# Layer 0's attention: one norm a slot earlier, two keys' products in slot 0, and the last mask turned inside the last projection

## The chip, the cores and the metric

The kernel runs on one core of a Trainium2 chip. A core has five engines that run side by side, each working through its own instructions in order: TensorE (PE in the profile; PEld are its weight loads), VectorE (DVE), ScalarE (ACT), GpSimd (POOL), and SyncE (SP), which here only issues DMA transfers. Engines wait for each other through semaphores. [...]

The metric is the device time of one execution in microseconds. For the kernel before, three runs were timed: 1245.64, 1251.21 and 1258.18 us, the median 1251.21.

## The reference, cut to what matters

A two-layer perceiver on 64 batches of 32 latent rows of 256 numbers. Each layer is a cross attention, an attention and a feed-forward part, each added to x. The change touches layer 0's attention and the work that is laid beside it: the choice of blocks for layer 0's feed-forward part, and that part's first group.

```python
def _L0_attn_ref(x, g_norm, Wq, Wkv, Wout, g_out):
    ...
    xn = _layernorm(x, g_norm)
    q = xn @ Wq
    kv = xn @ Wkv
    k, v = (kv[..., :DIM_HEAD], kv[..., DIM_HEAD:])
    q = q.reshape(B, N, HEADS, DIM_HEAD).transpose(0, 2, 1, 3)
    q = _l2norm(q * SCALE)
    k = _l2norm(k)
    ...
    sim = jnp.einsum('bhid,bjd->bhij', q, k)
    attn = jax.nn.softmax(sim.astype(jnp.float32), axis=-1).astype(sim.dtype)
    out = jnp.einsum('bhij,bjd->bhid', attn, v)
    out = out.transpose(0, 2, 1, 3).reshape(B, N, HEADS * DIM_HEAD)
    out = out @ Wout
    return _layernorm(out, g_out)

def _L0_ffn_ref(x, Wr, br, W1, W2):
    ...
    prob = jax.nn.softmax(xf @ Wr.T + br, axis=-1)
    _, idx = jax.lax.top_k(prob, TOP_K)
    mask = mask.at[jnp.arange(n)[:, None], idx].set(1.0)
    h = jnp.einsum('nf,ibf->nib', xf, W1b)
    h = jax.nn.gelu(h, approximate=False) * mask[:, :, None]
    y = jnp.einsum('nib,fib->nf', h, W2b)
    ...

x = x + _L0_xattn_ref(_layernorm(x, axis=-1), ctx_512, ...)
x = x + _L0_attn_ref(_layernorm(x, axis=-1), ...)
x = x + _L0_ffn_ref(_layernorm(x, axis=-1), ...)
```

There are 16 heads of 128; the mask keeps 4 of 16 blocks of 64 hidden units for each row.

## The kernel before

The 2048 rows of x lie in SBUF as 16 tiles `xs[0]` to `xs[15]` of 128 rows, in four groups of four (g = 0 to 3). Everything is float32. The program runs in stages, and each stage opens its own pools of SBUF and PSUM and closes them at its end: stage A (layer 0's cross attention), stage B (layer 0's attention, pools wB, psB and psB2), stage C (the rest of layer 0's feed-forward part and the weights of layer 1's cross attention, pools wC and psC), and the later ones. Pools that outlive a stage are const, xnp (four buffers of one normed tile, tag "xn"), xtp, small and mbp (the masks as they are multiplied).

In stage B the order on TensorE, VectorE, ScalarE and GpSimd is the order of the code; in stage C this holds for TensorE and ScalarE only, and the compile step orders the rest, as it orders SP's transfers everywhere here.

Stage B is a loop over slots t = 0 to 16. Slot t does, for tile t: `similar` (scores `Sb` and squared lengths `ssb`, L806 and L814, then a square root), `scale` (a reciprocal on VectorE, L828, and a product), `power` (exp on ScalarE, L834), `share` (the sum over the keys `denb` on TensorE, L840, then the reciprocal L842 and the product that makes `pTb`), and for tile t - 1: `gather` (`avb`, L853, needs pTb), `project` (16 heads, each one product of the output weights, `yb`, L866), `norm_stats` and `norm_out` (L884 to L886: VectorE reads yb in PSUM and writes `yn`, GpSimd multiplies by the gain and adds to x). Between them stand numbered places 0, 1, 2, 5, 3, 4 in this order; `at(slot, place, fn)` hangs further work there:

- `query_part` (places 0 to 3): the queries of later tiles, `qb`, L775, copied out by ScalarE.
- `keys_norm`, `keys_turn`, `keys_of`, `turn_keys` for group g: the normed latents, turned (`tp_b` into `xT_b`), multiplied by the key and value weights in two halves of two tiles (`kvp`, L340, copied and squared by ScalarE), and the keys turned (`kTp`).
- `choose_norm`, `choose_turn`, `choose_blocks`, `choose_best`, `choose_store` for groups 0 to 2: the choice of blocks. `choose_best` makes the mask on VectorE in four rounds of small operations; `choose_store` turns it with four transposes (`mTp`, L627), copies it to SBUF (`mTc`, L629) and stores it to DRAM (`maskd`, L630), from where `spread` reads it broadcast.
- `ln_group(0, "c")`, `ff_begin`, `ff_hidden`, `ff_output`: the first group of the feed-forward part. `ln_group` takes the statistics of four tiles on VectorE (two instructions a tile), a square root on ScalarE, and with act=True scales the tiles on ScalarE (L190).

Places 2 and 5 stand ahead of `project`; place 5 is behind `power`, and `share` is behind `project`. In slot 16 there is no new tile: it projects and norms tile 15 among the last feed-forward outputs of group 0. Last, `write_pad(t)` in every slot fills a part of a DRAM buffer with 1040 KB from the tile `pad`. After the loop `choose_store(2)` runs as step (17, 2).

Stage C begins with `hidden(1, 0)`: products `hp` (L644) into PSUM, gelu on ScalarE (L651) into `hc`, multiplied by the mask on VectorE (L652). The weights of layer 1's cross attention (`d_q` first, L1028) are loaded at its start.

Of the kernel before, what the change touches and what calls it, by code (L numbers as in the profile page):

```python
# [7 lines left out]
F32 = mybir.dt.float32  # L8
# [5 lines left out]
P = 128  # L14
B, S, D = 64, 32, 256
NT = B * S // P
NG = NT // 4
# [28 lines left out]
def perceiver_kernel(ctx: ExitStack, tc: tile.TileContext, a: dict, out: bass.AP):  # L46
# [3 lines left out]
    const = ctx.enter_context(tc.tile_pool(name="const", bufs=1))  # L50
    xtp = ctx.enter_context(tc.tile_pool(name="xtp", bufs=2))
    xnp = ctx.enter_context(tc.tile_pool(name="xnp", bufs=4))
# [14 lines left out]
    def sm(name, shape):  # L67
        return small.tile(shape, F32, tag=name.split("_")[0], name=name)
# [97 lines left out]
    def stats(mv_slot, src, name):  # L166
        st = sm(f"lnb_{name}", [P, 6])
        nc.vector.bn_stats(st, src)
        nc.vector.bn_aggr(mv_slot, st)

    def ln_scale(mv, name, twice=False, power=False):

        rs = rstd_of(mv, 4, name, power)
        if twice:

            v2 = sm(f"lnw_{name}", [P, 4, 2])
            nc.vector.tensor_tensor(v2[:, :, 1], mv[:, :, 1], rs, ALU.mult)
            nc.vector.tensor_tensor(v2[:, :, 1], v2[:, :, 1], rs, ALU.mult)
            rs2 = rstd_of(v2, 4, f"{name}b", power)
            nc.vector.tensor_tensor(rs2, rs2, rs, ALU.mult)  # L180
            rs = rs2
        sh = sm(f"lnh_{name}", [P, 4])
        nc.vector.scalar_tensor_tensor(sh, mv[:, :, 0], -1.0, rs, ALU.mult, ALU.mult)
        return rs, sh

    def ln_out(x_, rs, sh, i, name, act=False):

        y = xnp.tile([P, D], F32, tag="xn", name=f"xn_{name}_{i}")
        if act:
            nc.scalar.activation(  # L190
                y, x_, AF.Identity, scale=rs[:, i : i + 1], bias=sh[:, i : i + 1]
            )
        else:
            nc.vector.scalar_tensor_tensor(
                y,
                x_,
                rs[:, i : i + 1],
                sh[:, i : i + 1].to_broadcast([P, D]),
                ALU.mult,
                ALU.add,  # L200
            )
        return y

    def ln_group(g, name, twice=False, act=False, power=False):

        mv = sm(f"lnm_{name}{g}", [P, 4, 2])
        for i in range(4):
            stats(mv[:, i, :], xs[4 * g + i], f"{name}{g}_{i}")
        rs, sh = ln_scale(mv, f"{name}{g}", twice, power)
        return [ln_out(xs[4 * g + i], rs, sh, i, f"{name}{g}", act) for i in range(4)]  # L210
# [114 lines left out]
    def keys_norm(g):  # L325
        latT[g] = ln_group(g, "b", twice=True, act=True, power=g == 0)

    def keys_turn(g, ps):
        latT[g] = transposed(latT[g], ps, g, "b", gain=gn)

    def keys_of(g, ps, part):

        xT = latT[g]
        if part == 0:
            keys[g] = kvp.tile([P, 4, D], F32, tag="kv", name=f"kvb{g}"), sm(f"ssk_b{g}", [P, 4])
        kv, ssk = keys[g]
        for i in range(2 * part, 2 * part + 2):
            kv_ps = ps.tile([P, D], F32, tag="mm", name=f"kvp{g}_{i}")
            for k in range(KC):
                nc.tensor.matmul(  # L340
                    kv_ps,
                    xT[:, k, i * P : (i + 1) * P],
                    b_kv[:, k, :],
                    start=(k == 0),
                    stop=(k == KC - 1),
                )
            nc.scalar.copy(kv[:, i, :], kv_ps)
            junk = kvp.tile([P, P], F32, tag="junk", name=f"junkb{g}_{i}")
            nc.scalar.activation(junk, kv[:, i, :P], AF.Square, accum_out=ssk[:, i : i + 1])
        if part == 1:  # L350
            sk = sm(f"sk_b{g}", [P, 4])
            nc.scalar.activation(sk, ssk, AF.Sqrt, bias=keps, scale=1.0 / 16.0)
            rk = sm(f"rk_b{g}", [P, 4])
            nc.vector.reciprocal(rk, sk)
            for i in range(4):
                nc.vector.tensor_scalar_mul(kv[:, i, :P], kv[:, i, :P], rk[:, i : i + 1])
            keys[g] = kv
# [13 lines left out]
    with tc.tile_pool(name="wA", bufs=2) as work, tc.tile_pool(  # L371
        name="psA", bufs=1, space=PSUM
    ) as ps1, tc.tile_pool(
        name="psA2", bufs=2, space=PSUM
# [128 lines left out]
        def project(t):  # L503
            oT = ctxo.pop(t)
            y_ps = ps1.tile([P, D], F32, tag="o", name=f"ya{t}")
            for k in range(KC):
                nc.tensor.matmul(
                    y_ps, oT[:, k, :], a_o[:, k, :], start=(k == 0), stop=(k == KC - 1)
                )
            nc.vector.tensor_add(xs[t], xs[t], y_ps)  # L510
# [50 lines left out]
    def choose_norm(g, act=True):  # L561
        choice[g] = ln_group(g, "r", act=act)
# [59 lines left out]
    def choose_store(g, ps, work):  # L622

        mask = choice.pop(g)[2]
        mT_ps = ps.tile([16, 512], F32, tag="mm", name=f"mTp{g}")
        for i in range(4):
            nc.tensor.transpose(mT_ps[:, i * P : (i + 1) * P], mask[:, i, :], ident)  # L627
        mT = work.tile([16, 512], F32, tag="mT", name=f"mTc{g}", bufs=1)
        nc.vector.tensor_copy(mT, mT_ps)  # L629
        nc.sync.dma_start(maskd[g], mT)  # L630

# [94 lines left out]
    with tc.tile_pool(name="wB", bufs=2) as work, tc.tile_pool(  # L726
        name="psB", bufs=1, space=PSUM
# [134 lines left out]
        def project(t):  # L862
            oT = ctxo.pop(t)
            y_ps = outs[t] = ps1.tile([P, D], F32, tag="y", name=f"yb{t}")
            for h in range(NH):
                nc.tensor.matmul(  # L866
                    y_ps, oT[:, h, :], b_o[:, h, :], start=(h == 0), stop=(h == NH - 1)
                )

        def norm_stats(t):  # L870
            mv = sm(f"lnm_bo{t}", [P, 1, 2])
            stats(mv[:, 0, :], outs[t], f"bo{t}")
            ve = sm(f"lnv_bo{t}", [P, 1])
            nc.vector.tensor_scalar_add(ve, mv[:, :, 1], EPS)
            sd = sm(f"lns_bo{t}", [P, 1])
            nc.scalar.activation(sd, ve, AF.Sqrt)
            outs[t] = outs[t], mv, sd

        def norm_out(t):
            y_ps, mv, sd = outs.pop(t)  # L880
            rs = sm(f"lnr_bo{t}", [P, 1])
            nc.vector.reciprocal(rs, sd)
            yn = work.tile([P, D], F32, tag="yn", name=f"ynb{t}")
            nc.vector.tensor_scalar(yn, y_ps, mv[:, 0, 0:1], rs, ALU.subtract, ALU.mult)  # L884
            nc.gpsimd.tensor_tensor(yn, yn, vec[:, V_GOUT : V_GOUT + D], ALU.mult)
            nc.gpsimd.tensor_tensor(xs[t], xs[t], yn, ALU.add)  # L886
# [20 lines left out]
        steps = {}  # L907

        def at(slot, place, fn):
            steps.setdefault((slot, place), []).append(fn)  # L910

        for g in range(1, NG):
            at(4 * g - 4, 2, lambda g=g: keys_turn(g, ps2))
            at(4 * g - 3, 1, lambda g=g: keys_of(g, ps2, 0))
            at(4 * g - 3, 3, lambda g=g: keys_of(g, ps2, 1))
            at(4 * g - 2, 2, lambda g=g: turn_keys(g, ps2))
            if g > 1:
                at((3, 6)[g - 2], 5, lambda g=g: keys_norm(g))
        for g in range(NG - 1):
            at(4 * g + 5, 5, lambda g=g: choose_norm(g))  # L920
            at(4 * g + 6, 1, lambda g=g: choose_turn(g, ps2, work))
            at(4 * g + 7, 5, lambda g=g: choose_blocks(g, ps2, work))
            at(4 * g + 7, 5, lambda g=g: choose_best(g, work, (0, 1)))
            at(4 * g + 8, 5, lambda g=g: choose_best(g, work, (2, 3)))
            at(4 * g + 9, 2, lambda g=g: choose_store(g, ps2, work))
        ff, late = {}, []

        def ff_late():
# [21 lines left out]

        at(10, 4, lambda: ff.update(mb=spread(0)))
        at(16, 2, lambda: ff.update(mb1=spread(1)))
        at(11, 5, lambda: ff.update(xn=ln_group(0, "c", act=True)))
        at(12, 2, ff_begin)
        for f, (slot, place) in enumerate(
            ((13, 2), (13, 3), (14, 0), (14, 1), (14, 2), (14, 3), (15, 0), (15, 1))
# [7 lines left out]
        for t in range(NT + 1):  # L964
# [25 lines left out]
            if t > 0:  # L990
                project(t - 1)
                norm_stats(t - 1)
# [4 lines left out]
            if t > 0:  # L997
                norm_out(t - 1)
# [7 lines left out]
            write_pad(t)  # L1006
            if t in (2, 4):
                load_c(t // 4)
        for step in steps.get((NT + 1, 2), ()):
            step()  # L1010
        xT_c1 = ff["xT1"]


# [7 lines left out]
    with tc.tile_pool(name="wC", bufs=2) as work, tc.tile_pool(  # L1021
        name="psC", bufs=2, space=PSUM
# [150 lines left out]
        for g in range(1, NG):  # L1173
# [4 lines left out]
            if g == 1:  # L1178
                mb = spread(2)
                xn = ln_group(2, "c", power=True)  # L1180
# [3 lines left out]
            if g == 3:  # L1184
                xn = ln_group(0, "d", power=True)
# [31 lines left out]
    with mbw, wd1:  # L1217
# [3 lines left out]
        with tc.tile_pool(name="wD", bufs=2) as work, tc.tile_pool(  # L1221
            name="psD", bufs=1, space=PSUM
        ) as ps1, tc.tile_pool(
            name="psD2", bufs=2, space=PSUM
# [217 lines left out]
            steps, lat = {}, {}  # L1442
# [299 lines left out]
    with tc.tile_pool(name="wE", bufs=2) as work, tc.tile_pool(  # L1742
        name="psE", bufs=1, space=PSUM
# [7 lines left out]
        ps2 = ps1  # L1751
# [439 lines left out]
```

## Time and profile before

| What | us |
|---|---|
| median of three runs | 1251.21 |
| lowest, highest | 1245.64, 1258.18 |
| the profiled execution | 1262.62 |
| its span (first to last instruction) | 1260.7 |

| Stretch of the span (us) | what runs | TensorE busy (us) | granted clock |
|---|---|---|---|
| 0 to 139 | loads, stage A | 126.75 | 0.94 |
| 139 to 505 | stage B | 352.05 | 0.97 |
| 505 to 644 | stage C | 133.34 | 0.93 |
| 644 to 981 | layer 1's cross attention | 328.86 | 0.99 |
| 981 to 1122 | layer 1's attention and routing | 114.55 | 0.77 |
| 1122 to 1260.7 | layer 1's feed-forward part | 131.06 | 0.99 |

The slots of stage B begin where TensorE starts `Sb` for a tile: 151.99 (slot 0), 168.76, 190.52, 208.95, 226.94, 246.27, 267.87 (slot 6), 287.74, 307.51, 326.84, 348.88 (slot 10), 368.74, 388.52 (slot 12), 413.49, 432.41 and 453.25 (slot 15).

In the profile a line of a timeline gives start, duration, engine, code line, operation, what it writes and reads, the shape, and in brackets how long the engine had been idle before and what ended that. "Granted clock" is the share of TensorE's full clock that was let through, averaged over the stretch. A line of waits gives who waited for whom, the total, the number of times and the longest.

### The profile page before, as it was taken

What the parts mean: (1) busy time and instruction counts of PE and PEld (TensorE: products, weight loads), DVE (VectorE), ACT (ScalarE), POOL (GpSimd) and SP (SyncE); (2) the same over time, 40 slices, a digit from 0 to 9 for tenths busy, and PEclk for the clock granted to TensorE, in tenths of its full rate; (3) what the DMA queues carried; (4) which work ended last, traced back from release to release, by engine and by line L of the source; (5) the groups of instructions that cost most, each with busy time, mean ns of one, the idle gap of its engine ahead of it and who ended that gap; (6) DMA issues with size and microseconds to landing.
All of it is one profiled execution on the core that took longest, in us unless ns stands there. A gap on an engine that the chain in (4) does not pass through costs nothing. (4 is left out here: it accounts for less than half of the span.)

```text
span 1260.7 us, 26257 instructions
## 1 busy us (share of the span) xinstructions
PE 1186.6 (94%) x10187; PEld 832.7 (66%) x10187; DVE 775.8 (62%) x1885; ACT 557.9 (44%) x1305; POOL 368.6 (29%) x472
## 2 busy tenths in 40 slices
PE   8999999999999999999989999999999788789997
PEld 5656767677776557578667777776766466655664
DVE  5766247678869866443257777677775455665333
ACT  2437344464544541221346656565655355331111
POOL 2333326675766563100010000000010356332111
PEclk9989989999998989998989999999999888689999
DMA  5121124554463452832051111121200244211110
GB/s 148 42 70 36 28 76 118 157 155 119 119 185 108 116 165 76 257 104 63 25 116 31 47 37 47 39 53 30 53 1 1 94 145 162 66 39 56 43 33 10
DMA packets 94973, 103.11 MB, mean 82 GB/s; under 512 B 37792, under 2 KB 71329, under 8 KB 94626
## 3 DMA queue, kind: packets, MB, share of 16 engines
q1 hardware_dynamic: 92978, 97.19, 27.0%
q0 software_dynamic: 1872, 4.23, 1.0%
q8 instruction: 82, 1.34, 0.4%
q14 instruction: 41, 0.34, 0.1%
HBM read 69.45 MB, written 32.85 MB: 81 GB/s over the span
## 5 line engine op out<-in xcount | busy, mean ns | idle before, releaser
L1362 ACT ACTIVATE pp<-Sd,nm 128x257 f32<-128x257 f32 x256 | 118.0, 474 | 66.7 <-DVE nm L1358 61.4
L775 PE MATMUL qb<-xT_b,b_q 128*128 128x256 f32 x512 | 125.4, 394 | 0.0
L775 PEld LDWEIGHTS qb<-xT_b,b_q 128*128 128x128 f32 x512 | 97.4, 195 | 41.4 <-issue 20.9
L866 PE MATMUL yb<-b_o,oTb 128*128 128x256 f32 x512 | 116.4, 386 | 0.0
L866 PEld LDWEIGHTS yb<-b_o,oTb 128*128 128x128 f32 x512 | 98.6, 194 | 14.4 <-issue 0.7
L1358 DVE TENSOR_REDUCE nm<-Sd 128x2 f32<-128x514 f32 x128 | 83.1, 686 | 23.1 <-PE Sd L1350 23.1
L1371 DVE TENSOR_TENSOR pp<-pp,rd 128x514 f32<-128x514 f32 x128 | 89.0, 695 | 2.1
L1393 ACT COPY pTd<-pt 128x512 f32<-128x512 f32 x112 | 61.4, 598 | 49.6 <-PE pt L1387 49.6
L794 POOL TENSOR_TENSOR q2b<-qTb 128x512 f32<-128x512 f32 x64 | 65.2, 1046 | 28.2 <-ACT qTb L783 18.5
L1410 PE MATMUL od<-pTd,na 128*64 128x256 f32 x480 | 65.3, 392 | 5.6 <-issue 4.3
L783 ACT COPY qTb<-qb 128x512 f32<-128x512 f32 x64 | 37.4, 584 | 73.1 <-PE qb L775 71.5
L1350 PE MATMUL Sd<-ct,qTd 64*128 64x257 f32 x480 | 68.3, 403 | 0.0
L1387 PE MATMUL pt<-cst,pp 128*128 128x128 f32 x512 | 67.4, 275 | 0.0
L1387 PEld LDWEIGHTS pt<-cst,pp 128*128 128x128 f32 x512 | 59.4, 142 | 9.9 <-issue 5.6
L1148 PE MATMUL qd<-xT_d,d_m 128*128 128x256 f32 x256 | 65.3, 399 | 0.2 <-ACT xT_d L242 0.2
L828 DVE RECIPROCAL rqb<-rqb 128x512 f32<-128x512 f32 x16 | 53.5, 3343 | 17.8 <-ACT rqb L823 17.8
L657 PE MATMUL yc<-c,hc 128*128 128x256 f32 x256 | 59.7, 389 | 2.7 <-DVE hc L652 2.7
L1426 PE MATMUL yd<-d_n,co 128*128 128x256 f32 x256 | 59.5, 386 | 0.0
L1148 PEld LDWEIGHTS qd<-xT_d,d_m 128*128 128x128 f32 x256 | 47.2, 194 | 17.2 <-issue 6.0
L842 DVE RECIPROCAL rdb<-denb 128x512 f32<-128x512 f32 x16 | 53.7, 3355 | 6.7 <-PE denb L840 6.5
L657 PEld LDWEIGHTS yc<-c,hc 128*128 128x128 f32 x256 | 49.4, 196 | 12.2 <-DVE hc L652 3.5
L1426 PEld LDWEIGHTS yd<-d_n,co 128*128 128x128 f32 x256 | 47.3, 190 | 11.6 <-issue 5.8
(389 smaller groups left out, 2342.7 us busy)
## 6 DMA issues: line engine op xcount, KB each, us to landing
srt<-pad SPq DMA_DIRECT2D x17, 1040.0 KB
mb<-maskd SPq DMA_DIRECT2D x64, 128.0 KB
ct<-ctd SPq DMA_DIRECT2D x30, 257.0 KB
rct<-in_ctxT_dram SPq DMA_DIRECT2D x32, 128.5 KB
rrt<-in_ctxT_dram SPq DMA_DIRECT2D x64, 64.2 KB
ctd<-rct SPq DMA_DIRECT2D x32, 128.5 KB
nad<-rna SPq DMA_DIRECT2D x16, 256.0 KB
fw<-in_f_wg_dram SPq DMA_DIRECT2D x8, 512.0 KB
```

The costliest lines, as they stand in the source:

```text
L657: nc.tensor.matmul(y_ps, hs[f][:, i * P : (i + 1) * P], c_2[:, f, :], start=(f == 0), stop=(f == 7),)
L775: nc.tensor.matmul(q_ps[:, hh, :], b_q[:, k, h * P : (h + 1) * P], xT[:, k, c0 : c0 + 256], start=(k == 0), stop=(k == KC - 1),)
L794: nc.gpsimd.tensor_tensor(q2[:, 4 * h4 : 4 * h4 + 4, :], q, q, ALU.mult)
L866: nc.tensor.matmul(y_ps, oT[:, h, :], b_o[:, h, :], start=(h == 0), stop=(h == NH - 1))
L1148: nc.tensor.matmul(q_ps[:, r, :], m[:, k, pr * P : (pr + 1) * P], xT[:, k, c0 : c0 + 256], start=(k == 0), stop=(k == KC - 1),)
L1350: nc.tensor.matmul(s_ps[:, hh, :NKV], qT[hs, b % 8, 4 * u : 4 * u + 4, :], ct[hs, b % 4, :], start=True, stop=True,)
L1358: nc.vector.tensor_reduce(nm, s_ps[:, :, :NKV], AX.X, ALU.max, negate=True)
L1362: nc.scalar.activation(pp[:, hh, :], s_ps[:, hh, :NKV], AF.Exp, bias=nm[:, hh : hh + 1], accum_out=sd[:, hh : hh + 1],)
L1371: nc.vector.tensor_tensor(pp, pp, bc(rd, 2, NKV), ALU.mult)
L1387: nc.tensor.transpose(pt[:, hh * 256 + u * P : hh * 256 + u * P + P], probs[b][:, u, hh, c * P : (c + 1) * P], ident,)
L1410: nc.tensor.matmul(o_ps[64 * hh : 64 * hh + 64, 0, :], na[:, j, c, :], pT[:, c, hh * 256 : (hh + 1) * 256], start=(c == 0), stop=(c == 1),)
L1426: nc.tensor.matmul(y_ps, co[:, pr, :], n[:, pr, :], start=(pr == 0), stop=False)
```

## The change

Three moves, and what they need:

1. `keys_of(1, part 0)`, the key and value products of the first two tiles of group 1, goes from slot 1, place 1, to slot 0, place 5.
2. `ln_group(0, "c")`, the norm for group 0's feed-forward part, goes from slot 11, place 5, to slot 10, place 5.
3. `choose_store(2)` goes from behind the loop into the last projection: after head 11 of tile 15, before heads 12 to 15. Its tile `mTc` is taken from const rather than from the stage's work pool (in all groups), and the last `yn` from xnp rather than from the work pool.

```diff
-        mT = work.tile([16, 512], F32, tag="mT", name=f"mTc{g}", bufs=1)
+        mT = const.tile([16, 512], F32, tag="mT", name=f"mTc{g}", bufs=1)
...
                     y_ps, oT[:, h, :], b_o[:, h, :], start=(h == 0), stop=(h == NH - 1)
                 )
+                if (t, h) == (NT - 1, 11):
+                    choose_store(NG - 2, ps2, work)
...
-            yn = work.tile([P, D], F32, tag="yn", name=f"ynb{t}")
+
+            last = t == NT - 1
+            yn = (xnp if last else work).tile(
+                [P, D], F32, tag="xn" if last else "yn", name=f"ynb{t}"
+            )
...
-            at(4 * g - 3, 1, lambda g=g: keys_of(g, ps2, 0))
+            slot, place_ = (0, 5) if g == 1 else (4 * g - 3, 1)
+            at(slot, place_, lambda g=g: keys_of(g, ps2, 0))
...
-            at(4 * g + 9, 2, lambda g=g: choose_store(g, ps2, work))
+            if g < NG - 2:
+                at(4 * g + 9, 2, lambda g=g: choose_store(g, ps2, work))
...
-        at(11, 5, lambda: ff.update(xn=ln_group(0, "c", act=True)))
+        at(10, 5, lambda: ff.update(xn=ln_group(0, "c", act=True)))
...
-        for step in steps.get((NT + 1, 2), ()):
-            step()
```

## The prediction

> **What bounds the kernel now.** I read the page's totals first, then the waits of TensorE alone from 140 to 520 us (layer 0's attention and its end), then the timeline of TensorE around each wait, then the stretches with the granted clock.
>
> ```profile
> PE 1186.6 (94%) x10187; PEld 832.7 (66%) x10187; DVE 775.8 (62%) x1885; ACT 557.9 (44%) x1305; POOL 368.6 (29%) x472
> ```
>
> TensorE is busy for 94% of the span, so time comes off only where it waits or runs at a low clock. Its waits in the stage (total, times, longest):
>
> ```profile
> PE hp L644 <- DVE mTc L629: 3.3, 1, 3.3
> PE denb L840 <- ACT pTb L834: 2.7, 1, 2.7
> PE yc L657 <- DVE hc L652: 2.7, 2, 1.7
> PE avb L853 <- DVE pTb L843: 2.5, 1, 2.5
> PE hp L644 <- ACT hc L651: 1.6, 1, 1.6
> ```
>
> All but the third (slot 15, untouched) are what the change aims at: 10.1 us. What each wait costs beyond itself, by the timeline (start, duration, instructions):
>
> ```profile
> 163.35 2.07 PE L840 MATMUL denb<-pTb,cst 128*128 128x512 f32 x2 [2.72 <-ACT pTb L834]
> 165.21 3.62 PE L775 MATMUL qb<-xT_b,b_q 128*128 128x256 f32 x8
> 186.04 1.02 PE L840 MATMUL denb<-pTb,cst 128*128 128x512 f32 x2
> 186.90 1.89 PE L775 MATMUL qb<-xT_b,b_q 128*128 128x256 f32 x8
> ...
> 394.86 2.09 PE L853 MATMUL avb<-pTb,kvb 32*128 32x512 f32 x8 [2.48 <-DVE pTb L843]
> 396.88 5.86 PE L775 MATMUL qb<-xT_b,b_q 128*128 128x256 f32 x16
> ...
> 500.82 0.60 PE L627 MATMUL mTp<-cst,maskc 128*16 128x128 f32 x4
> 504.74 6.51 PE L644 MATMUL hp<-xT_c,c 128*128 128x512 f32 x8 [3.33 <-DVE mTc L629]
> 512.86 10.57 PE L644 MATMUL hp<-xT_c,c 128*128 128x512 f32 x24 [1.60 <-ACT hc L651]
> ```
>
> After each of the three long waits the same work takes twice its time (denb 2.07 against 1.02, qb 3.62 against 1.89). The stretches with the granted clock (the number before the DMA share) say why; slot 0 and its end, then slot 1:
>
> ```profile
> 152.00:169.00 17.00, 14.04 (x63) 9.17 (x66) 7.48 (x4) 7.63 (x11) 11.91 (x12) 0.80 0.25 68
> 169.00:190.50 21.50, 21.50 (x106) 15.80 (x98) 10.31 (x11) 11.56 (x22) 2.08 (x2) 1.00 0.19 58
> ```
>
> A mean of 0.80 over 17 us is 2 x 0.20 x 17 = 6.8 us at half clock, which costs some 3 us beyond the wait. Slot 12 shows 0.86 over 25 us and the stage's border 0.89 over 25.3: much the same. At the stage's end three further rows matter:
>
> ```profile
> 503.00 0.53 DVE L884 TENSOR_SCALAR ynb<-yb,lnm_bo,lnr_bo 128x256 f32<-128x256 f32 x1
> 503.92 0.68 DVE L629 COPY mTc<-mTp 16x512 f32<-16x512 f32 x1
> 504.62 0.34 SPq L630 DMA_DIRECT2D maskd<-mTc  x1
> 510.73 0.38 SPq L1028 DMA_DIRECT2D d_q<-in_d_wq_dram  x1
> 510.92 1.28 ACT L651 ACT_TABLE_LOAD   x1 [8.46 <-DVE lnv_r L159]
> ```
>
> hp reads neither mask nor mTc, yet starts 0.14 us after the copy to mTc: the next stage's first PSUM tile waits for the last reader of the stage's PSUM. The gelu (table load at 510.92) and the d_q load (510.73) start together, though hp's first tile was done near 508. Between lies only the DMA traffic of 506.5 to 510.6, the 1040 KB pad store with mTc's store behind it. So I read the wait named lnv_r as that store landing: mTc lies in the closing work pool, whose space both need.
>
> **Part 1, keys_of(1, part 0) from slot 1 to slot 0, place 5.** No DMA, no POOL: 8 matmul passes (1.80 us start to start: 175.60 to 177.40) and on ScalarE two times 0.37 + 0.31 + 0.19. They can start when the second turned xT_b is copied (160.66 + 0.69, so about 161.45) and end near 163.3, just as denb is released (163.35). TensorE's idle falls to 0.24 + 0.87 us and the clock should hold. Slot 1 then starts at 163.35 + 0.86 + 1.72 = 165.93 (spacing of slot 1's own denb and qb) instead of 168.76: 2.83. Slot 1 loses the passes, 1.80, and its slow start, 0.15. **4.8 us.** ScalarE's 1.74 us follow exp and fit before 165.9; its next copy now waits until 168.87. If the clock would have held anyway, only the 1.80 remain; that is the low end.
>
> **Part 2, ln_group(0, "c") from slot 11 to slot 10.** No DMA, no POOL. On VectorE 386.99 to 389.98, 3.0 us standing before slot 11's reciprocal (390.73); on ScalarE one square root and four scalings (2.07). Without it rdb starts at about 387.75, after denb (386.86), and pTb ends at 391.8; TensorE reaches avb at 392.4. No wait: slot 12 (388.52 to 413.49, 24.97) becomes like slot 8 (307.51 to 326.84, 19.33), which follows slot 7 with the same block choice and no norm. **5.6 us**, of which 2.5 is the wait and 3.1 the clock. The margin is only 0.6 us, so the low end is 2.5. In slot 10 VectorE waits 6.21 us for the projection (360.05 to 366.27) and ScalarE 4.39: the norm is hidden there. If that cover were gone it would cost its 3.0 again. Behind it in VectorE's order stand norm_stats and the reciprocal; avb waits for them.
>
> [...] In slot 11 POOL had stopped (385.3) before the norm; in slot 10 it squares queries from 361.3 to 365.3. The trace's nearest row is slot 6, keys_norm under the same squares: statistics 0.39 to 0.42 as elsewhere, but two 4-element operations took 0.93 and 0.97 for 0.17. [...] By the rows 0 to 2 us more; 3.0 + 2.0 still ends 1 us before 366.27. So nothing is charged.
>
> **Part 3, the last mask.** The four transposes (0.44 start to start, as kTp) move before the last four heads. choose_best ends 4.35 us after the projection begins (498.25 − 493.91); head 12 comes at three quarters of 7.07 = 5.3: 0.95 us to spare, no stall. The 0.68 copy moves ahead of norm_stats into idle VectorE time; its store moves past the pad store on SP and past norm_out's two POOL operations, in const, so nothing waits for it. yn in xnp frees the work pool from POOL's last two operations. What is late next: hp now waits for L884, the last PSUM reader. The projection ends 0.44 later, so L884 ends at 503.53 + 0.44 = 503.97 and hp starts at 504.11, only 0.63 sooner. An idle of 2.69 us lies between the 2.48 and the 2.72 that halved the clock, so I take the half clock: two tiles take 6.51, to 510.6. The gelu, free of the store, is done by 504.11 + 3.25 + 1.28 + 0.60 = 509.2, so the third tile starts at 510.6, not 512.86. **2.2 us.** With a full clock the gelu sets it (504.11 + 1.73 + 1.28 + 0.65 = 507.8): 5.1. If stage C's statistics are put ahead of L884, as some already are (501.37 to 502.67), 0 or below: each costs 0.4, a run of five 2 us, so −2 to 5.1. The d weights load 6 us earlier; nothing waits for them (first use 538.9).
>
> [...] By the page the waits bring only 1.8 + 2.5 + 5.1 = 9.4; by the rows the sum is 4.8 + 5.6 + 2.2 = **12.6**. The rows decide.
>
> The profiled execution took 1262.6 us (span 1260.7) and would take 1250.0. It lies 11.4 above the median, 1251.2, so some half-clock stretches may be missing from the median run; I keep the sum: 1251.2 − 12.6 = **1238.6**.
>
> **Rivals.** (a) The clock does not follow: the waits go, but part of the slow stretches were absent or return one slot on. Gain 1.8 + 2.5 + 2.2 = 6.5, 1244.7. For it: the runs spread over 12.5 us. Against: all three waits here were followed by it. (b) The border stays shut: L884 falls behind stage C's statistics, part 3 gives −2 to 0; gain 9.4, 1241.8. For: VectorE's order there is not written by hand. (c) Slower: the re-planned order of engines after 981 us. There (981 to 1122) the clock averages 0.77, which is 65 us at half speed, and TensorE is busy 114.6 of 141. [...] Against: nothing in the diff touches that stretch. (d) The border runs at full clock: 15.5, 1235.7.
>
> **Chances.** The sum 0.50, (a) 0.17, (b) 0.12, (c) 0.08, (d) 0.13. A measurement tells about 1% (12.5 us) from no change, and the sum lies on that line: half of its chance and a little more (0.29), (d) whole and a share of (a) and (b) make faster 0.47; same 0.45; slower 0.08. Range 1229 (full clock everywhere with a lucky median) to 1250 (all low ends).
>
> **What would show it.** Right: denb in slot 0 at about 1.0 with a wait under 1 us; no wait at slot 12's avb, whose slot takes 19.4; slot 10 unchanged at 19.9; hp released by L884 and a gelu right behind its first tile; d_q issued near the pad store. Wrong: a wait of mTp on maskc within the projection; a wait moved to slot 10's denb or avb; hp starting no sooner after the projection than 3.3 us.

## The result and the profile after

The changed kernel takes 1247.30 us in the median (1237.77 to 1251.38, 22 runs) against 1255.78 us of the kernel before (1245.64 to 1261.75, 22 runs): a ratio of 0.9934, 95% interval 0.9918 to 0.9950. That is 8.3 us less (6.3 to 10.3), where the prediction's sum had 12.6. The change is faster, but by less than 1%, which the forecast held slightly less likely than more than 1%. The forecast time, 1238.6, was 8.7 below the measured one; about half of that is the starting point, since over 22 runs the kernel before has a median 4.6 above that of the first three.

The profiled execution took 1249.61 us, its span 1247.6. The page's totals:

```profile
PE 1178.9 (94%) x10187; PEld 827.1 (66%) x10187; DVE 777.5 (62%) x1885; ACT 557.9 (45%) x1305; POOL 367.9 (29%) x472
```

TensorE's busy time is 7.7 us below that of the first profile, with the same number of instructions. That is not the change's doing alone: in four profiles of the kernel before it lies between 1168.7 and 1186.6, in three of the changed kernel between 1170.7 and 1178.9. Its waits from 130 to 520 us (total, times, longest), longest first; the last two lines are what is left of two that were 2.7 and 1.6:

```profile
PE hp L644 <- DVE ynb L890: 2.7, 1, 2.7
PE yc L657 <- DVE hc L652: 2.6, 2, 1.7
...
PE denb L840 <- ACT pTb L834: 0.4, 1, 0.4
PE hp L644 <- ACT hc L651: 0.4, 1, 0.4
```

The wait for pTb is gone, that for mTc is gone, and at the border the wait for the last norm (L884 before, L890 now) has taken its place, as forecast (the same line of code; the diff moved it down). TensorE around the three places, in the timeline:

```profile
163.46 2.41 PE L340 MATMUL kvp<-b_kv,xT_b 128*128 128x256 f32 x8
166.25 1.13 PE L840 MATMUL denb<-pTb,cst 128*128 128x512 f32 x2 [0.38 <-ACT pTb L834]
167.21 1.89 PE L775 MATMUL qb<-xT_b,b_q 128*128 128x256 f32 x8
...
390.60 1.14 PE L853 MATMUL avb<-pTb,kvb 32*128 32x512 f32 x8
...
490.10 0.60 PE L627 MATMUL mTp<-cst,maskc 128*16 128x128 f32 x4
490.54 1.89 PE L866 MATMUL yb<-b_o,oTb 128*128 128x256 f32 x8
495.12 5.06 PE L644 MATMUL hp<-xT_c,c 128*128 128x512 f32 x8 [2.69 <-DVE ynb L890]
500.56 10.57 PE L644 MATMUL hp<-xT_c,c 128*128 128x512 f32 x24 [0.38 <-ACT hc L651]
```

denb takes 1.13 and the queries behind it 1.89, full speed (granted clock 1.00 from 155 to 190 us). Slot 0 takes 14.14 us and slot 1 19.80 (33.94 together, 38.53 before), slot 12 takes 19.33 (24.97), slot 10 is unchanged at 19.86. mTp does not wait for the mask. From the start of the last projection to the first hp tile 10.20 (10.84), to the third 15.64 (18.95). In these two executions stage B up to the third hp tile is 15.2 us shorter: more than the sum, and nearly twice what the runs show. The rest of the document is about that gap.

### The profile page after: what moved, and what is told of

It is laid out like the page before. It is cut to its first block, busy times and chain, and to the rows that moved or that the text cites. A ratio compares the mean times of both kernels' runs of the same rounds, so it can differ in the third digit from the quotient of the medians.

```text
span 1247.6 us, 26254 instructions
## 1 busy us (share of the span) xinstructions
PE 1178.9 (94%) x10187; PEld 827.1 (66%) x10187; DVE 777.5 (62%) x1885; ACT 557.9 (45%) x1305; POOL 367.9 (29%) x472
## 5 line engine op out<-in xcount | busy, mean ns | idle before, releaser
L775 PE MATMUL qb<-xT_b,b_q 128*128 128x256 f32 x512 | 122.0, 387 | 0.0
L794 POOL TENSOR_TENSOR q2b<-qTb 128x512 f32<-128x512 f32 x64 | 64.7, 1040 | 27.0 <-ACT qTb L783 15.7
```

Source lines behind the costliest of these rows:

```text
L775: nc.tensor.matmul(q_ps[:, hh, :], b_q[:, k, h * P : (h + 1) * P], xT[:, k, c0 : c0 + 256], start=(k == 0), stop=(k == KC - 1),)
L794: nc.gpsimd.tensor_tensor(q2[:, 4 * h4 : 4 * h4 + 4, :], q, q, ALU.mult)
```

## The experiments

A slot is measured from `Sb` to `Sb` on TensorE, the border from the start of the last projection to the third hp tile. Ratios are to the kernel before on the same chip, with their 95% interval.

**Part 1 alone**

```diff
+            slot, place_ = (0, 5) if g == 1 else (4 * g - 3, 1)
+            at(slot, place_, lambda g=g: keys_of(g, ps2, 0))
```

> Part 1 alone (the keys' first products in slot 0). The sum says 4.8 us less: slots 0 and 1 together 33.8 instead of 38.5, denb behind a wait under 1 us and at about 1.0. The rival that the half clock follows such a wait in only a part of the executions says between 1.8 and 4.8 in the median, with the same trace. The rival that time is given back later says 4.8 less by the trace of slots 0 and 1, but a median that moves by 1 us or less, and a longer stretch behind stage B.

0.9980 (0.9963 to 0.9998), 2.5 us (0.3 to 4.7). Slots 0 and 1 take 33.93. The time lies between the two ends, 1.8 and 4.8, as the rival of a clock that does not always follow said.

**Part 2 alone**

```diff
-        at(11, 5, lambda: ff.update(xn=ln_group(0, "c", act=True)))
+        at(10, 5, lambda: ff.update(xn=ln_group(0, "c", act=True)))
```

> Part 2 alone (the norm in slot 10). The sum says 5.6 us less: slot 12 at 19.3 instead of 25.0, slot 10 unchanged at 19.9. The rival of a half clock that comes by chance says 2.5 to 5.6 in the median with the same trace; the rival of time given back later says the same trace and a median that moves by 1 us or less.

0.9961 (0.9936 to 0.9985), 4.9 us (1.9 to 8.0, so the times alone do not tell the sum's 5.6 from the low end of 2.5). Slot 12 takes 19.32, slot 10 19.86. In this execution slot 0, which part 2 leaves alone, took 15.82, not 16.77, at a granted clock of 0.90 over 17 us, not 0.80: the first sign that the waits of before are not always followed by the same slow stretch.

**Part 3 alone**, with all its edits of mTc, yn and the place of `choose_store`:

> Part 3 alone (the mask turned inside the last projection, mTc in const, the last yn in xnp). From the start of the last projection to the third tile of hp 18.95 us before; the sum says 16.7 (2.2 less), hp released by the norm's L884 after about 2.7 us. With a full clock behind that wait 13.9 (5.1 less). If stage C's statistics are put ahead of L884, 19 or more. The median should move by 2.2 to 5.1.

0.9943 (0.9923 to 0.9963) over six runs, 7.2 us; the border takes 14.25, with hp at full clock (4.05 for its first two tiles). The 7 us are more than its trace shows; it was timed again below.

**The kernel before, unchanged**, profiled a second time:

> The kernel before once more, for a second profile of it. If the half clock follows a wait by chance, at least one of the three waits (slot 0, slot 12, the border) is followed by work at full speed here: denb at 1.0 behind its 2.7, slot 12 near 22, or the first two hp tiles in about 3.5. If it follows always, all three are slow again: slots 0 and 1 together 38.5, slot 12 25.0, the border 18.95.

Its timeline at slot 0 and slot 12:

```profile
162.83 1.12 PE L840 MATMUL denb<-pTb,cst 128*128 128x512 f32 x2 [2.72 <-ACT pTb L834]
163.80 1.89 PE L775 MATMUL qb<-xT_b,b_q 128*128 128x256 f32 x8
...
391.55 1.14 PE L853 MATMUL avb<-pTb,kvb 32*128 32x512 f32 x8 [2.48 <-DVE pTb L843]
392.62 3.72 PE L775 MATMUL qb<-xT_b,b_q 128*128 128x256 f32 x16
```

The same waits, 2.72 and 2.48 to the digit, and behind them full speed: denb 1.12 instead of 2.07, avb 1.14 instead of 2.09. Slot 0 takes 14.13, slot 12 21.88. The border still takes 18.95.

**Two more profiles of it**

> The kernel before, a third profile. By the account that the half clock follows these waits by chance, slot 0 takes 14.1, 15.8 or 16.8, slot 12 21.9, 23.5 or 25.0, and not always the highest; by the sum as predicted always 16.8 and 25.0.

> The kernel before, a fourth profile. As for the third: by chance of the clock slot 0 takes 14.1, 15.8 or 16.8 and slot 12 takes 21.9, 23.5 or 25.0; by the sum always the highest of them.

Slot 0 took 16.77 and 15.83, slot 12 21.90 and 21.89, the border 18.95 and 17.70. The stretch from 152 to 169 us, by windows (the number ahead of the DMA share is the granted clock), in the second profile of the kernel before and then in the third:

```profile
152.00:169.00 17.00, 14.04 (x81) 9.20 (x74) 8.43 (x6) 9.65 (x13) 12.42 (x12) 1.00 0.26 71
```

```profile
152.00:169.00 17.00, 14.04 (x66) 9.10 (x62) 8.30 (x5) 7.74 (x11) 11.37 (x12) 0.80 0.27 73
```

One program, one wait, and a clock of 1.00 or 0.80.

**The wait of slot 12 filled, with the norm left in slot 11**

```diff
-                for k in range(KC):
+                for k in list(range(KC)) * (2 if n_ == AHEAD + 48 else 1):
```

> The kernel before, with the first query products of slot 12 computed twice (1.9 us of TensorE inside its wait for pTb; the norm stays in slot 11). The wait shrinks to about 0.5 us and avb starts no sooner. If the half clock behind the wait is what the profile of before shows, slot 12 takes 21.9 instead of 25.0 and never more; the median gains the chance of the half clock times 3.1, so 0 to 3. If the slow work had another cause (the late copies on ScalarE), slot 12 stays at 25 or goes to 27.

0.9996 (0.9974 to 1.0018). The wait fell to 0.77 and slot 12 took 21.89; but the kernel before takes that in most profiles too, so this one tells nothing of the clock. By its interval, what the halving behind that wait is worth in the median is at most about 3 us. Inconclusive.

**The changed kernel again**

> The changed kernel once more. If part of the gain comes by chance of the clock, stage B shows the same slots 0, 1 and 12 (14.1, 19.8, 19.3) as in its first profile, while stage A (151 to 155) and the border (13.9 to 16.7) move with the clock. Gain in the median 6 to 10.

0.9928 (0.9905 to 0.9950), 9.0 us. Slots 14.13, 19.80, 19.33; border 15.68; stage A ended at 151.9 instead of 154.9.

**mTc in const and nothing else**

```diff
-        mT = work.tile([16, 512], F32, tag="mT", name=f"mTc{g}", bufs=1)
+        mT = const.tile([16, 512], F32, tag="mT", name=f"mTc{g}", bufs=1)
```

> The kernel before, with mTc in const and nothing else. If the long wait of the gelu and of d_q is the store of the mask out of the closing pool, both start now behind GpSimd's last addition to x (yn still lies in the pool) or the first hp tile: d_q about 6 us sooner after the last projection, the gelu about 3, the third hp tile 17.0 to 17.7 after the last projection's start instead of up to 18.95. hp itself starts as before (10.8). If the wait is for something else, 18.95 and d_q unchanged.

ScalarE's first gelu, then SyncE's transfers in the timeline of this kernel:

```profile
500.64 1.28 ACT L651 ACT_TABLE_LOAD   x1 [4.39 <-PE hp L644]
```

```profile
498.42 0.34 SPq L630 DMA_DIRECT2D maskd<-mTc  x1
498.99 0.97 SPq L1028 DMA_DIRECT2D d_q<-in_d_wq_dram  x1
```

The gelu now waits for its hp tile, and d_q goes out 0.6 us behind the mask's store; before it was 6.1. So the wait that the profile named lnv_r was the landing of that store. The border took 14.88, lower than expected because hp ran at full clock (its first eight products in 3.67, against 6.51 in the first profile of before); three profiles with mTc in the work pool and hp at full clock as well show 17.70, 17.71 and 18.94. hp itself still starts at 10.84.

**Part 3 and the whole change, timed side by side**

> Part 3 alone, timed again beside the whole change. If the traces are right it gains 2 to 5 us in the median (0.996 to 0.998) and the border takes 14 to 16; if part 3 really brings 7 (0.994), it is as fast as the whole change here, and parts 1 and 2 bring nothing together with it.

> The whole change, timed beside part 3 alone on the same chip: 0.991 to 0.995 as before, 4 to 7 us faster than part 3 alone if the parts add up, the same as part 3 alone if they do not.

Part 3: 0.9969 (0.9944 to 0.9995), 3.9 us, border 14.25. The whole: 0.9948 (0.9923 to 0.9973), 6.5 us, border 14.25. The earlier 7 us of part 3 were not repeated. The intervals of the two overlap, so the times do not show that parts 1 and 2 add something to part 3, nor that the parts add up: timed alone they give 2.5, 4.9 and 7.2 or 3.9. That each of them holds within the whole is read from the slots.

**Going on: one output of stage B behind the last projection**

```diff
-        ... ((15, 2), (15, 3), (16, 0), (16, 1))
+        ... ((15, 2), (15, 3), (16, 0), (16, 4))
```

> The changed kernel, with the last feed-forward output of group 0 (yc, 3.5 us of TensorE) moved from in front of the last projection to behind it, into the wait for the norm. The stage's end then waits for the addition of that output (0.45 and 0.1), not for L884: wait at the border 0.6 instead of 2.7, the clock holds, so 2.1 to 4 less than the changed kernel from S of slot 15 to the third hp tile. The rival: the mask or the copies of oT come too late once this cover is gone, and a wait of 1 to 2 appears at the last projection's start or at mTp.

0.9932 (0.9905 to 0.9959): nothing over the changed kernel (0.9928 on the same chip), where 2.1 to 4 us were expected. The rival came, and more. Its waits:

```profile
PE hp L644 <- DVE x L664: 2.6, 1, 2.6
PE mTp L627 <- DVE maskc L620: 1.0, 1, 1.0
PE yb L866 <- DVE mxc L607: 0.4, 1, 0.4
```

The work that moved had been the mask's cover, so mTp now waits for it; and the addition L664 that releases hp stands in VectorE's order behind an instruction of stage C:

```profile
487.79 0.17 DVE L183 SCALAR_TENSOR_TENSOR lnh_c<-lnm_c,lnr_c 128x4 f32<-128x4 f32 x1 [2.03 <-POOL lnr_c L156]
487.87 0.24 DVE L169 BATCH_NORM_AGGREGATE lnm_r<-lnb_r 128x2 f32<-128x6 f32 x2
488.03 0.39 DVE L664 TENSOR_TENSOR x<-x,yc 128x256 f32<-128x256 f32 x1
```

It waits 2.03 there for GpSimd. So the mechanism of the prediction's rival (b) is real, at another instruction than feared.

**The first two outputs behind slot 15's projection as well** (slots and places (15, 3), (15, 3), (16, 0), (16, 4)):

> As the kernel with the last output moved, and the first two outputs of group 0 go behind slot 15's projection as well, so that TensorE does not wait there for hc (1.7 and 1.0 in the trace, with half a clock behind it). 2.6 to 6 less again between S of slot 15 and the last projection. The rival: the norm and block choice of slot 15 on VectorE are then too late, and the wait moves to denb or avb.

0.9900 (0.9871 to 0.9928). The waits for hc are gone and a wait of 3.0 for L664 at the third output has taken their place, since VectorE reaches slot 15's reciprocal late. Not clearly faster than the changed kernel.

**Part 2's step once more, for group 1**

```diff
-        ... ((15, 2), (15, 3), (16, 0), (16, 1))
+        ... ((15, 3), (15, 3), (16, 0), (16, 1))
...
-        at(15, 5, lambda: ff.update(xn1=ln_group(1, "c", act=True)))
+        at(14, 5, lambda: ff.update(xn1=ln_group(1, "c", act=True)))
```

> The changed kernel, with the same treatment for group 1: ln_group(1, "c") from slot 15 to slot 14 (VectorE idle 4.8 there before the projection, ScalarE 3.9, the norm 3.0 and 2.1), and the first two outputs of group 0 behind slot 15's projection, where they cover the reciprocal. TensorE no longer waits for hc (1.7 and 1.0), and pTb is 3 us earlier, so the third output does not wait for a PSUM buffer. From S of slot 15 to the last projection 34.9 to 35.5 instead of 39 to 41: 3.5 to 5.5 less than the changed kernel, of which 2.6 is certain. If the block choice on VectorE still is too late, a wait of up to 3 stays at the third output and the gain is 1 or less.

> The changed kernel with group 1's norm a slot sooner and two outputs behind slot 15's projection, a second time: 0.985 to 0.991 of the kernel before, 4 to 8 us less than the changed kernel on the same chip, no wait for hc in slot 15.

0.9876 (0.9846 to 0.9906) and 0.9874 (0.9846 to 0.9901): about 16 us less than the kernel before. On the chip where both were timed its interval ends at 0.9901, and that of the changed kernel begins at 0.9923: there it is faster, by 9.7 us between the medians, where 4 to 8 were expected. From `Sb` of slot 15 to the last projection it takes 32.82 and 34.40, against 38.99 to 40.64 in the changed kernel. The two edits, the norm and the two outputs, were not run apart. In its timeline of TensorE the three outputs run on without a wait:

```profile
458.87 1.02 PE L840 MATMUL denb<-pTb,cst 128*128 128x512 f32 x2
459.72 10.56 PE L657 MATMUL yc<-c,hc 128*128 128x256 f32 x48
470.21 1.14 PE L853 MATMUL avb<-pTb,kvb 32*128 32x512 f32 x8
```

## Why the prediction was right and wrong

The step that failed is "the rows decide": each wait was charged, for every execution, with the half clock that one profile showed behind it. This clock term was put at 3.0 us in part 1 and 3.1 in part 2; over the profiles it is worth 1.5 and 0.6 in the mean. Part 3 erred the other way, by 1.2. The waits themselves, and who ends them, were read rightly. The profiles of all kernels that leave a part out give the distribution (us):

| | without the part | with it | gain, mean | predicted |
|---|---|---|---|---|
| slot 0 | 14.13 or 14.14 twice, 15.82 or 15.83 five times, 16.76 and 16.77; mean 15.66 | 14.14 | 1.5 | 2.8 |
| slot 1 | 21.60 in most | 19.80 | 1.8 | 2.0 |
| slot 12 | 21.88 to 21.92 six times, 23.52, 24.97; mean 22.48 | 19.33 | 3.2 | 5.6 |
| border | 17.21 to 18.95 seven times; mean 18.17 | 14.25 three times, 15.64, 15.68; mean 14.81 | 3.4 | 2.2 |

(Slot 12 leaves out the kernel with the filled wait, the border that with mTc alone.) The sum of the means is 9.9, within the interval of the result (6.3 to 10.3); the three timings of the whole change give 8.3, 9.0 and 6.5. The profile of before was the only one of eight with the full price at slot 12, and one of two in nine with it at slot 0: that the prediction had just this one to go by was bad luck, that it took one profile for all was not.

- **Part 1.** The keys start when xT_b is copied and end as denb is released: shown, with 0.38 of wait left. The certain part, 1.8 for slot 1, came out. The clock term, taken as some 3, is 1.5 in the mean. Its low end of 1.8 was written down with the condition, and the sum then used the other end.
- **Part 2.** The wait of 2.48 is gone for good and slot 12 equals slot 8. In slot 10 the norm took 3.4 us of VectorE's idle time with 2.90 to spare; the small operation L183 took 0.16 among POOL's squares (359.58 to 363.62), as it did in slot 11 before (0.17), and not the 0.93 and 0.97 of slot 6. The clock term of 3.1 is 0.6 in the mean (22.48 against 21.89 without half clock): the term mis-sized the most.
- **Part 3.** hp starts 0.63 sooner, as predicted, released by the last norm. No wait at the mask. The gelu stands right behind its tile. Here the sum was too low: it set 6.5 at half clock for the first two tiles, which took 4.05 in three of five profiles and 5.44 or 5.48 in two; and its 18.95 before was the highest of seven. Also the old border was held by the store at 17 to 19 whatever the clock was, so this part is the least a matter of chance; the single edit of mTc already brings most of it (14.88 in its one profile).
- **Rivals.** (a), the clock does not follow in part of the executions, is what happened; the measured 8.3 lies nearer to its 6.5 than to the sum. (b) did not occur in the change. (c) did not: from the third hp tile to the end the profiles of before take 744.2 to 747.9, those of the changed kernel 744.1 to 747.0. (d), a full clock at the border, is what three of the five profiles with part 3 show.
- **What the rows of the granted clock show.** Around slot 0's wait the first profile of the kernel before has, in two stretches (length, busy time of TensorE, and again the clock ahead of the DMA share):

```profile
158.90:162.31 3.41, 1.49 (x10) 0.92 (x8) 0.04 (x1) 2.80 (x4) 3.25 (x4) 1.00 0.35 77
162.31:165.72 3.41, 2.37 (x4) 1.25 (x5) 0.26 (x1) 0.97 (x2) 1.83 (x2) 0.50 0.56 161
```

and the second profile:

```profile
158.22:161.63 3.41, 1.66 (x11) 1.08 (x9) 0.21 (x1) 2.64 (x4) 3.25 (x5) 1.00 0.34 77
161.63:165.05 3.42, 2.22 (x8) 1.61 (x9) 1.05 (x1) 1.14 (x2) 1.98 (x2) 1.00 0.51 155
```

In the first, TensorE is idle for 1.92 us (3.41 less 1.49) of one stretch, and the clock of the next is half; it stays at 0.50 to 169.13, 6.82 us in all, and is 1.00 from there to 190. In the second, with the same wait, the two stretches hold 1.75 and 1.20 us of idle time and the clock stays full. By the lengths in the table, slot 0's wait was followed by slow work in seven of nine profiles and slot 12's in two of eight. What decides in which of them was not shown: no run changed it.
- **The smaller sum.** The prediction's 9.4 was nearer to the 8.3 than its 12.6, but not by its terms: it left the clock out of parts 1 and 2, where it is worth 1.5 and 0.6 in the mean, and had 5.1 at the border, where the profiles give 3.4.

## What to carry to other kernels

Charge a wait with its own length first, and what the clock adds behind it only with the share of profiles in which it appears (here seven of nine behind 2.72 us, two of eight behind 2.48): profile the kernel before two or three times, for one profile may hold every bad case at once. Parts 1 and 2 took the clock's share away by shortening the wait: with 0.38 us left in slot 0 and none in slot 12, these slots took 14.14 and 19.33 in the profiles with them. A buffer that lies in a closing pool and is read by a late transfer can hold back what the next stage writes there: here d_q went out 6.1 us behind the store of mTc, and 0.6 us behind it with mTc in a longer-lived pool, a cheap move that does not depend on chance. Before moving work out of a place, look at what it was covering, and look for the same pattern elsewhere: the norm one slot sooner worked a second time and, together with the two outputs moved behind the projection, brought as much again as the whole change.

## What the runs showed of the hardware

- Behind a wait of 2.72 us on TensorE the granted clock over 17 us was 1.00 in one profile and 0.80 in two others, with the same program. In the first profile of before it was 0.50 from 162.31 to 169.13.
- The stretch up to the first `Sb`, whose instructions are the same in all these kernels, took between 148.5 and 154.9 us, a spread larger than what each of the three parts brought in the mean: 148.5 to 152.0 in 12 profiles, 153.5 to 154.9 in five. Two of the three profiles of the changed kernel had the longer one, none of the four of the kernel before. The 22 runs of one kernel spread over 14 to 16 us.
- A wait put down to lnv_r was the landing of a 32 KB store behind a 1040 KB one: 6.1 us from the store's issue to d_q's.
